# Four residual stages and an attention layer on one core: second sums computed already turned, adapters that hold the identity, and most value products moved to the end of the first part

## The chip, the cores and the metric

The kernel runs on one core of a Trainium2 chip. The metric is the device time of the whole kernel in microseconds (us). All numbers are float32. The engines are PE (TensorE, matrix products), DVE (VectorE), ACT (ScalarE), POOL (GpSimd) and SP (SyncE, which here only starts transfers). Each works through its own queue in order and waits on semaphores for the others.

## What is computed

The input x has 32 sequences of 32 rows of 512 numbers. Four residual steps follow each other:

```
x = x + mix(x)        # per sequence: a 32x32 matrix, picked by number, over the rows
x = x + x @ W.T + 0.5 * (x @ A[label]) @ Bw.T     # low rank 32, A picked among 5
x = x + x @ adapter[id].T                          # per sequence: a 512x512 matrix
x = x + attention(x)  # q, k, v projections, norm, rotation, cached pages, output
```

Below, x1, x2 and x3 are the values after the first, second and third step. The 1024 rows are handled as 8 tiles of 128 rows (4 sequences each).

## The kernel before

The kernel has three parts. The first makes x3 from x. The second makes queries, keys and values from x3; it goes by blocks of seven large products (`m`, L393) with everything around them on the other engines. The third is the attention. The change lies in the first part, and in the first chunk of value products (`project(NCH - 2, t)`, L312), which fill in there.

On PE a product needs the operand that is summed over on the partitions (the 128 rows of SBUF, the on-chip memory), so each x has to be had *turned*, with its 512 columns on the partitions in four pieces of 128 (`KC` = 4). In the first part PE does for each tile t:

- `mix(t)` (L688): four products of x with a 128x128 matrix `md` that holds the four sequences' mixing matrices and the identity. The result is x1 already turned (`x1t`); ACT copies it out of PSUM, the memory that PE writes.
- `low_1(t)` (L707): x1 times all five low-rank matrices `la`. DVE picks the tile's one (`picked`, L711, and a sum, L718) into `low`, a 128x128 tile of which 32 columns are used and the rest are zero.
- `base(t)` (L726): x1 times `wb`, which is W with the identity added on its diagonal (L850, four DVE adds at the start). It takes four matmuls of 512 columns, and gives x2 *not turned*, rows on the partitions. Ahead of the last one PE turns `low` (L729), ACT scales it by 0.5 (`lowt`, L731), and a fifth matmul of 512 columns (L732) adds the low-rank term with `lb`, of which 96 of 128 rows are zero. DVE copies the sum to `xs` (L734).
- `flip_2(t)` (L697): four transposes on PE that give `x2t`, and an ACT copy.
- `adapt(t)` (L751): 16 matmuls, for each of the four pieces one for each sequence, of 32 output rows beside each other, with the sequence's adapter `wa`, 1 MB each. DVE adds the result to `xs` (L758), which is x3.
- `transposed(t, x3t)` (L697): four transposes that turn x3, and an ACT copy. After each second tile POOL forms four sums of x3 (`token_sums`, L375 to L378) that the second part needs.

The tiles overlap: a loop over n gives `mix(n)`, `base(n-1)`, `flip_2(n-2)`, `low_1(n)`, the turning of x3 for tile n-4 and `adapt(n-3)`, and from n = 6 a value product of a finished tile. The order on PE and DVE in this part is that of the program text (`manual_schedule`); ACT, POOL and SP are ordered by the scheduler.

Adapters are loaded by SP, in order, into eight buffers (two tiles' worth). The loads of tile t+2 are issued after `adapt(t)`, which frees their buffers. Among them stand the weights of the value products (`wq`, after tile 3) and of the first pair of the second part (`w_pair`, after tile 5). SP's transfers use eight semaphores in turn, so that at most eight are under way.

`angles()` (L764 to L783) forms the angles of the rotation: some 18 DVE operations, three sines on ACT, and eight products on POOL (L789 to L792) into `cw` and `sw`, used from the second part's first block on. It stands right after `adapt(0)`. `constants()` (L136 and others) stands with it.

PSUM in this part: a pool `ps_m` of four banks, `ps_n` of two and `ps_tr` of two. `accumulator` gives every third sum of `base` and `adapt` to `ps_n`; `low_1` and the value products take `ps_m`. A new tile in a pool waits until the reader of the one that had its bank is done.

At the end of the part POOL stores `xs` to `x_d` (L891). Value products are copied out by ACT into two buffers (`vs`, L322) and stored from POOL's queue (L327).

## Time and profile before

| | us |
|---|---|
| median of 3 runs | 1136.51 |
| lowest and highest | 1135.58, 1136.70 |
| the profiled execution | 1136.3 |
| its span (first to last instruction) | 1134.5 |
| PE busy in the span | 1119.1 (99%) |
| DVE, ACT, POOL busy | 812.3, 739.3, 561.0 |
| start of the first product of the second part (`m`, L393) | 121.66 |
| `adapt(0)` to `adapt(7)` start on PE | 31.14, 42.17, 53.61, 64.64, 79.10, 95.01, 103.04, 114.11 |

The page gives busy time by engine, the span in 40 slices, the DMA queues, the chain of waits that ended last, the costliest groups of instructions, and the transfers. The time line lists instructions of an engine in order: start, duration, engine, line, operation, output and inputs, shape, and how many are merged in the row ("x8"; a float32 matmul is two entries). In square brackets stands how long the engine had been idle and what ended that. A matmul's listed duration overlaps the next, so its cost in a stream is read from the starts.

### The profile page before, as it was taken

What the parts mean: (1) busy time and instruction counts of PE and PEld (TensorE: products, weight loads), DVE (VectorE), ACT (ScalarE), POOL (GpSimd) and SP (SyncE); (2) the same over time, 40 slices, a digit from 0 to 9 for tenths busy, and PEclk for the clock granted to TensorE, in tenths of its full rate; (3) what the DMA queues carried; (4) which work ended last, traced back from release to release, by engine and by line L of the source; (5) the groups of instructions that cost most, each with busy time, mean ns of one, the idle gap of its engine ahead of it and who ended that gap; (6) DMA issues with size and microseconds to landing.
All of it is one profiled execution on the core that took longest, in us unless ns stands there. A gap on an engine that the chain in (4) does not pass through costs nothing.

```text
span 1134.5 us, 19093 instructions
## 1 busy us (share of the span) xinstructions
PE 1119.1 (99%) x5480; PEld 738.0 (65%) x5480; DVE 812.3 (72%) x1674; ACT 739.3 (65%) x1885; POOL 561.0 (49%) x730
## 2 busy tenths in 40 slices
PE   8999999999999899999999999999999999999998
PEld 5554444444444688777777777777777777777766
DVE  2510688887877578878778878887877787877861
ACT  1211377676666677678877777777777877777850
POOL 3411689899798455543444344334433443344410
PEclk9999999999999999999999999999999999999999
DMA  8998447688886687778767756775777676766600
GB/s 319 391 419 352 177 130 211 162 246 221 210 234 176 203 267 264 254 255 301 241 210 243 260 190 212 264 244 183 234 239 240 199 234 223 253 201 212 231 28 10
DMA packets 173355, 259.24 MB, mean 229 GB/s; under 512 B 31522, under 2 KB 130466, under 8 KB 168770
## 3 DMA queue, kind: packets, MB, share of 16 engines
q1 hardware_dynamic: 152226, 184.22, 51.4%
q0 software_dynamic: 20016, 71.97, 17.8%
q10 hardware_dynamic: 1008, 1.84, 0.4%
q8 instruction: 44, 0.72, 0.3%
q14 instruction: 61, 0.50, 0.1%
HBM read 228.46 MB, written 37.88 MB: 235 GB/s over the span
## 4 chain that ended last, share of the span: by engine, by line
PE 61%; DVE 2%; ACT 0%; issue 0%; DVEq 0%
PE o_ps L1103 19%; PE f_ps L1180 18%; PE s_ps L1023 11%; PE s_ps L1024 9%; PE o_ps L1123 2%; PE pn_ps L1090 1%; PE f_ps L1200 1%; PE f_ps_last L1200 1%; DVE placed L1079 1%; PE qkv L312 1%; DVE pr L1032 0%; DVE turned L1061 0%; ACT placed L1075 0%; DVE os L1139 0%; DVE ot L1160 0%
## 5 line engine op out<-in xcount | busy, mean ns | idle before, releaser
L1075 ACT COPY placed<-turned 32x512 f32<-32x512 f32 x524 | 322.6, 616 | 30.2 <-DVE turned L1061 24.2
L1103 PEld LDWEIGHTS o_ps<-vt,placed 128*128 128x128 f32 x2048 | 264.2, 191 | 110.9 <-issue 74.6
L1032 DVE CUSTOM_DVE_ANT_0 pr<-s_ps,mask,rq 128x544 f32<-128x544 f32 x256 | 200.4, 783 | 129.6 <-PE s_ps L1024 106.4
L1048 ACT ACTIVATE pr<-pr,low 128x544 f32<-128x544 f32 x256 | 191.6, 748 | 142.6 <-DVE low L1032 116.1
L1077 POOL COPY placed<-turned 32x512 f32<-32x512 f32 x279 | 169.6, 608 | 222.2 <-DVE turned L1061 173.5
L1103 PE MATMUL o_ps<-vt,placed 128*128 128x128 f32 x2048 | 272.0, 276 | 3.9 <-DVE os L1139 3.3
L1180 PE MATMUL f_ps<-wo,ot 128*128 128x512 f32 x480 | 240.6, 593 | 0.0
L1061 DVE STREAM_TRANSPOSE turned<-pr 128x512 f32<-128x512 f32 x256 | 178.6, 698 | 0.1
L1023 PE MATMUL s_ps<-kt,qt 128*128 128x288 f32 x512 | 174.0, 421 | 4.2 <-DVE low L1032 2.4
L1024 PE MATMUL s_ps<-kt,qt 128*128 128x256 f32 x512 | 152.3, 379 | 0.0
L252 POOL DMA_INDIRECT vt<-in_v_cache_dram,v_idx x128 | 124.3, 971 | 36.6 <-issue 25.7
L1024 PEld LDWEIGHTS s_ps<-kt,qt 128*128 128x128 f32 x512 | 97.3, 190 | 26.8
L438 POOL TENSOR_TENSOR ra<-ra,rs 128x512 f32<-128x512 f32 x80 | 103.8, 1303 | 10.7 <-DVE rs L433 8.1
L1079 DVE COPY placed<-turned 32x512 f32<-32x512 f32 x221 | 101.9, 461 | 5.6
L1180 PEld LDWEIGHTS f_ps<-wo,ot 128*128 128x128 f32 x480 | 86.9, 190 | 25.1 <-issue 13.9
L1086 POOL COPY pq<-pr 128x128 f32<-128x128 f32 x64 | 18.5, 288 | 151.6 <-ACT pr L1048 111.2
L1023 PEld LDWEIGHTS s_ps<-kt,qt 128*128 128x128 f32 x512 | 78.2, 191 | 17.3 <-DVE low L1032 6.1
L451 ACT ACTIVATE sq<-x 128x128 f32<-128x128 f32 x256 | 76.2, 301 | 19.8 <-DVE x L409 13.6
L548 ACT COPY r<-m 128x512 f32<-128x512 f32 x80 | 46.3, 579 | 52.4 <-PE m L393 50.4
L393 PE MATMUL m<-t_pair,x_sums 128*128 128x512 f32 x160 | 75.4, 594 | 0.7 <-ACT r L548 0.7
L393 PE MATMUL m<-w_pair,x3t 128*128 128x512 f32 x160 | 75.2, 592 | 0.0
L393 PE MATMUL m<-w_pair,x_sums 128*128 128x512 f32 x160 | 72.1, 593 | 0.0
(129 smaller groups left out, 1231.8 us busy)
## 6 DMA issues: line engine op xcount, KB each, us to landing
kt<-in_k_cache_dram SPq DMA_DIRECT2D x512, 128.0 KB
wa<-in_w_adapt_dram SPq DMA_DIRECT2D x32, 1024.0 KB
q_d<-st SPq DMA_DIRECT2D x128, 128.0 KB
qt<-q_d SPq DMA_DIRECT2D x64, 256.0 KB
w_pair<-in_w_qkv_dram SPq DMA_DIRECT2D x20, 512.0 KB
o_d<-in_w_o_dram SPq DMA_DIRECT2D x16, 512.0 KB
wo<-o_d SPq DMA_DIRECT2D x16, 512.0 KB
k_d<-st SPq DMA_DIRECT2D x32, 128.0 KB
```

The costliest lines, as they stand in the source:

```text
L252: nc.gpsimd.indirect_dma_start(out=vts[b][:, c, :], out_offset=None, in_=v_cache, in_offset=bass.IndirectOffsetOnAxis(ap=v_idx[:, at : at ...
L393: nc.tensor.matmul(ps, of[:, k], by[:, k], start=(not more and k == 0), stop=(k == KH - 1), skip_group_check=more,)
L1023: nc.tensor.matmul(ps[:, first:L], q, kt4[:, :N_LOW, g, :], start=True, stop=True)
L1024: nc.tensor.matmul(ps[:, L : first + LT], q, kt4[:, N_LOW:, g, :], start=True, stop=True)
L1032: nc.vector.tensor_tensor_reduce(pr, ps[:, first : first + LT], mask, rqs[b][:, g // QUAD, u : u + 1], 3.0e38, ALU.add, ALU.min, low,)
L1048: nc.scalar.activation(pr, pr, AF.Exp, bias=low, scale=-1.0, accum_out=dens[quad][:, u : u + 1])
L1061: nc.vector.transpose(part, pr)
L1075: nc.scalar.copy(dst, src)
L1077: nc.gpsimd.tensor_copy(dst, src)
L1079: nc.vector.tensor_copy(dst, src)
L1103: nc.tensor.matmul(po, pt[:, c, :], vt[:, c, g * D : (g + 1) * D], start=(c == 0 and q == 0), stop=(c == L // P - 1 and q == 1),)
L1180: nc.tensor.matmul(pfs[t][:, :HID], ots[t, h // HALF][:, h % HALF, :], wo(h), start=(h == 0), stop=(h == (HQ if t < NT - 1 else HALF) - 1),)
```

## The change

- `base(g)` works on two tiles at once with the operands exchanged: `wb` is loaded as the weights and x1 turned (256 columns, two tiles) streams. The result is x2 *turned*, in four banks of `ps_m`. `flip_2` and its four transposes per tile go; four ACT copies of 256 columns per pair make `x2t`.
- The low-rank term: `low` holds the 32 columns four times (one DVE copy more), turned and scaled for two tiles, and four matmuls, each with 32 rows of `lb` and of `lowt` at another partition (four row groups), add it to the four banks. `lb` comes in four transfers of 16 KB.
- Since x2 is no longer had with rows on the partitions, the adapters get the identity added: `with_identity(t)`, two DVE adds for each adapter (128x384 and 128x128), so that `adapt` gives x3 itself. DVE copies it to `xs`; the copy of x2 goes.
- The order is written out by hand. `angles()` moves from after `adapt(0)` to after `adapt(3)`, behind the adds of tile 4 and ahead of `mixed(6, 7)`. Of the value products one stands after `adapt(3)`, one after `adapt(4)`, the others after `adapt(6)` and `adapt(7)`. `wq` is loaded after tile 2's adapters, the first pair after tile 7's.
- `low_1`, `adapt` and the value products of this part now share the two banks of `ps_n`. Three memsets and that of `lb` go; `mg` and `md` have one buffer more.

On DVE the order around the moved part is: copy of `adapt(3)`, adds of tile 4, `angles`, picks of `low_1(6)` and `low_1(7)`, copy of `adapt(4)`, adds of tile 5. In `ps_n`, `adapt(4)` takes the bank of `low_1(6)`.

```diff
-        def base(t: int):
-            xt = x1ts.pop(t)
-            pb = accumulator(f"base_{t}")
-            for k in range(KC):
-                nc.tensor.matmul(pb, xt[:, k, :], wb[:, k, :], start=(k == 0), stop=False)
...
-            nc.tensor.matmul(pb, lowt, lb, start=False, stop=True)
-
-            nc.vector.tensor_copy(xs[:, t, :], pb)
-
-        def flip_2(t: int):
-            x2ts[t] = sp.tile([P, KC, P], F32, tag="x2t", name=f"x2t_{t}")
-            transposed(t, x2ts[t], "x2t")
+        def base(g: int):
+            xt = x1ts.pop(g)
+            pbs = [
+                ps_m.tile([P, HID], F32, tag="mm", name=f"base_{g}_{j}")[:, : 2 * P]
+                for j in range(KC)
+            ]
+            lowt = sp.tile([P, 2 * P], F32, tag="lowt", name=f"lowt_{g}")
+            for j in range(KC):
+                for k in range(KC):
+                    nc.tensor.matmul(
+                        pbs[j],
+                        wb[:, k, j * P : (j + 1) * P],
+                        xt[:, k, :],
+                        start=(k == 0),
+                        stop=False,
+                    )
+                if j == KC - 2:
+                    plt = ps_tr.tile([P, 2 * P], F32, tag="tr", name=f"lowt_ps_{g}")
+                    for u in range(2):
+                        low = lows.pop(2 * g + u).rearrange("p j r -> p (j r)")
+                        nc.tensor.transpose(plt[:, u * P : (u + 1) * P], low, ident)
                     nc.scalar.mul(lowt, plt, LORA_SCALING)
+            x2ts[g] = sp.tile([P, KC, 2 * P], F32, tag="x2t", name=f"x2t_{g}")
+            for j in range(KC):
+                r = slice(j * R, (j + 1) * R)
+                nc.tensor.matmul(pbs[j], lb[r, :], lowt[r, :], start=False, stop=True)
+            for j in range(KC):
+                nc.scalar.copy(x2ts[g][:, j, :], pbs[j])
...
+        def with_identity(t: int):
+            for b in range(t * BT, (t + 1) * BT):
+                w = was[b].rearrange("p k o -> p (k o)")
+                step = HID + P
+                most = w[:, : (KC - 1) * step].rearrange("p (k o) -> p k o", o=step)[:, :, :P]
+                last = w[:, (KC - 1) * step :]
+                one = ident.unsqueeze(1).to_broadcast([P, KC - 1, P])
+                nc.vector.tensor_tensor(most, most, one, ALU.add)
+                nc.vector.tensor_tensor(last, last, ident, ALU.add)
...
-            pa2 = accumulator(f"adapt_{t}")
+            pa2 = ps_n.tile([P, HID], F32, tag="mm", name=f"adapt_{t}")
...
-            nc.vector.tensor_tensor(xs[:, t, :], xs[:, t, :], pa2, ALU.add)
+            nc.vector.tensor_copy(xs[:, t, :], pa2)
...
+            base(0)
+            with_identity(0)
+            mixed(2, 3)
+            adapt(0)
+            loads(2)
...
+            base(2)
+            turned(2)
+            adapt(3)
+            loads(5)
+            with_identity(4)
+            values_of(0)
+            angles()
+            mixed(6, 7)
+            turned(3)
+            adapt(4)
+            loads(6)
+            with_identity(5)
+            values_of(1)
+            turned(4)
+            adapt(5)
+            loads(7)
+            with tc.issue_after(picked[-1]):
+                load_pair(0)
+            with_identity(6)
+            base(3)
+            turned(5)
+            adapt(6)
+            with_identity(7)
+            values_of(2)
+            values_of(3)
+            turned(6)
+            adapt(7)
+            values_of(4)
+            values_of(5)
+            turned(7)
+            values_of(6)
```

`mixed(6, 7)` is `mix` of both tiles and then `low_1` of both; `turned(t)` is the turning of x3 with POOL's sums after each odd tile; `values_of(t)` is a value product.

More of the change, by code (lines that the diff above doesn't have):

```diff
@@ L287, in cond_resid_kernel @@
     ps_tr = flips.enter_context(tc.tile_pool(name="a_tr", bufs=2, space=PSUM, side="right"))
-    taken = []
-    def accumulator(name: str, long: bool = False):
-        taken.append(name)
-        pool = ps_m if long or len(taken) % 3 else ps_n
-        return pool.tile([P, HID], F32, tag="mm", name=name)
     x3_all = xp.tile([P, KC, NT * P], F32, name="x3t")
@@ L327, in store_values, with project @@
         eng.dma_start(out=v_d[t * P : (t + 1) * P, c0 : c0 + HID], in_=vs)
-    def project(c: int, t: int, slots=()):
-        ps = accumulator(f"qkv_{c}_{t}", True)
+    def project(c: int, t: int, slots=(), pool=ps_m):
+        ps = pool.tile([P, HID], F32, tag="mm", name=f"qkv_{c}_{t}")
         for k in range(KC):
@@ L638, in cond_resid_kernel @@
         la = w1p.tile([P, KC, NL * R], F32, name="la")
-        lb = w1p.tile([P, HID], F32, name="lb")
-        nc.gpsimd.memset(lb, 0.0)
+        lb = w1p.tile([P, P], F32, name="lb")
         ones = w1p.tile([P, HID], F32, name="ones")
@@ L651, in cond_resid_kernel @@
         mgs, x1ts, lows, x2ts, was = {}, {}, {}, {}, {}
-        wide = [w1p.tile([P, P], F32, name=f"low_{i}") for i in range(3)]
-        for low in wide:
-            nc.gpsimd.memset(low, 0.0)
         def gather_mix(t: int):
-            mg = sp.tile([P, S], F32, tag="mg", name=f"mg_{t}", bufs=4)
+            mg = sp.tile([P, S], F32, tag="mg", name=f"mg_{t}", bufs=5)
             nc.gpsimd.indirect_dma_start(
@@ L670, in mixers @@
         def mixers(t: int):
-            md = sp.tile([P, BT, S], F32, tag="md", name=f"md_{t}", bufs=3)
+            md = sp.tile([P, BT, S], F32, tag="md", name=f"md_{t}", bufs=4)
             nc.vector.tensor_tensor(
@@ L690, in mix @@
                 )
-            x1ts[t] = sp.tile([P, KC, P], F32, tag="x1t", name=f"x1t_{t}", bufs=3)
-            nc.scalar.copy(x1ts[t], px)
+            g, u = divmod(t, 2)
+            if u == 0:
+                x1ts[g] = sp.tile([P, KC, 2 * P], F32, tag="x1t", name=f"x1t_{g}")
+            nc.scalar.copy(x1ts[g][:, :, u * P : (u + 1) * P], px)
         def transposed(t: int, dst: bass.AP, name: str):
@@ L704, in low_1 @@
         def low_1(t: int):
-            plo = ps_m.tile([P, HID], F32, tag="mm", name=f"low_ps_{t}")[:, : NL * R]
+            g, u = divmod(t, 2)
+            plo = ps_n.tile([P, HID], F32, tag="mm", name=f"low_ps_{t}")[:, : NL * R]
             for k in range(KC):
                 nc.tensor.matmul(
-                    plo, x1ts[t][:, k, :], la[:, k, :], start=(k == 0), stop=(k == KC - 1)
+                    plo,
+                    x1ts[g][:, k, u * P : (u + 1) * P],
+                    la[:, k, :],
+                    start=(k == 0),
+                    stop=(k == KC - 1),
                 )
@@ L716, in low_1 @@
             )
-            lows[t] = wide[t % 3]
+            lows[t] = sp.tile([P, KC, R], F32, tag="low", name=f"low_{t}")
             nc.vector.tensor_reduce(
-                lows[t][:, :R], picked.rearrange("p l r -> p r l"), AX.X, ALU.add
+                lows[t][:, 0, :], picked.rearrange("p l r -> p r l"), AX.X, ALU.add
             )
-        def base(t: int):
-            xt = x1ts.pop(t)
-            pb = accumulator(f"base_{t}")
-            for k in range(KC):
-                nc.tensor.matmul(pb, xt[:, k, :], wb[:, k, :], start=(k == 0), stop=False)
-                if k == KC - 2:
-                    plt = ps_tr.tile([P, P], F32, tag="tr", name=f"lowt_ps_{t}")
-                    nc.tensor.transpose(plt, lows.pop(t), ident)
-                    lowt = sp.tile([P, P], F32, tag="lowt", name=f"lowt_{t}")
-                    nc.scalar.mul(lowt, plt, LORA_SCALING)
-            nc.tensor.matmul(pb, lowt, lb, start=False, stop=True)
-            nc.vector.tensor_copy(xs[:, t, :], pb)
@@ L736, in flip_2 @@
-        def flip_2(t: int):
-            x2ts[t] = sp.tile([P, KC, P], F32, tag="x2t", name=f"x2t_{t}")
-            transposed(t, x2ts[t], "x2t")
+            nc.vector.tensor_copy(
+                lows[t][:, 1:, :], lows[t][:, 0, :].unsqueeze(1).to_broadcast([P, KC - 1, R])
+            )
[12 more added lines that the diff above has]
+                        xt[:, k, :],
+                        start=(k == 0),
+                        stop=False,
+                    )
+                if j == KC - 2:
[3 more added lines that the diff above has]
+                        nc.tensor.transpose(plt[:, u * P : (u + 1) * P], low, ident)
+                    nc.scalar.mul(lowt, plt, LORA_SCALING)
+            x2ts[g] = sp.tile([P, KC, 2 * P], F32, tag="x2t", name=f"x2t_{g}")
[4 more added lines that the diff above has]
+                nc.scalar.copy(x2ts[g][:, j, :], pbs[j])
@@ L742, in load_adapt @@
             dma_picked(was[b], w_adapt, pk[0:1, b : b + 1], "a p k o -> p (a k) o")
+        def with_identity(t: int):
[7 more added lines that the diff above has]
+                nc.vector.tensor_tensor(last, last, ident, ALU.add)
         def adapt(t: int):
-            xt = x2ts.pop(t)
-            pa2 = accumulator(f"adapt_{t}")
+            g, u = divmod(t, 2)
+            xt = x2ts[g][:, :, u * P : (u + 1) * P]
+            pa2 = ps_n.tile([P, HID], F32, tag="mm", name=f"adapt_{t}")
             for k in range(KC):
@@ L781, in angles @@
             nc.vector.scalar_tensor_tensor(turns, af, -1.0, af, ALU.mult, ALU.max)
-            cs = w1p.tile([P, NT, H2], F32, name="cs")
-            nc.scalar.activation(
-                cs.rearrange("p t f -> p (t f)"), turns, AF.Sin, bias=half_pi, scale=-1.0
-            )
+            cs = ang
+            nc.scalar.activation(af, turns, AF.Sin, bias=half_pi, scale=-1.0)
             for i in range(2):
@@ L803, in cond_resid_kernel @@
         load_x(2)
-        nc.sync.dma_start(out=lb[:R, :], in_=lora_b)
+        for j in range(KC):
+            nc.sync.dma_start(
+                out=lb[j * R : (j + 1) * R, :], in_=lora_b[:, j * P : (j + 1) * P]
+            )
         load_x(3)
@@ L827, in cond_resid_kernel, with mixed, ahead_of, loads @@
                 nc.tensor.matmul(idle[:, :n], ones[:, :P], ones[:, :n], start=True, stop=True)
-            def ahead_of(t: int):
-                if t + 3 < NT:
-                    gather_mix(t + 3)
-                if t < NT:
-                    mixers(t)
-            def adapt_and_load(t: int):
-                adapt(t)
-                if t + 2 < NT:
-                    for j in range(BT):
-                        load_adapt((t + 2) * BT + j)
+            def mixed(*tiles):
+                for t in tiles:
+                    mix(t)
+                for t in tiles:
+                    low_1(t)
+            def ahead_of(*tiles):
+                for t in tiles:
+                    if t + 3 < NT:
+                        gather_mix(t + 3)
+                    mixers(t)
+            def loads(t: int):
+                for j in range(BT):
+                    load_adapt(t * BT + j)
+            def turned(t: int):
+                transposed(t, x3t(t), "x3t")
+                if t % 2:
+                    token_sums(t // 2)
+            def values_of(t: int):
+                project(NCH - 2, t, (), ps_n)
             ahead_of(0)
@@ L852, in cond_resid_kernel @@
             low_1(1)
+            ahead_of(3)
             base(0)
-            mix(2)
-            low_1(2)
-            ahead_of(3)
-            flip_2(0)
-            base(1)
-            for n in range(3, NT + 4):
-                if n < NT:
-                    mix(n)
-                if n - 1 < NT:
-                    base(n - 1)
-                if n - 2 < NT:
-                    flip_2(n - 2)
-                if n < NT:
-                    low_1(n)
-                    ahead_of(n + 1)
-                if NT <= n:
-                    project(NCH - 2, n - 6 + (n == NT + 3))
-                if n == NT + 2:
-                    project(NCH - 2, NT - 3)
-                if 0 <= n - 4 < NT:
-                    transposed(n - 4, x3t(n - 4), "x3t")
-                    if n % 2:
-                        token_sums((n - 4) // 2)
-                if n - 3 < NT:
-                    adapt_and_load(n - 3)
-                if n == 3:
-                    constants()
-                    angles()
-                if 6 <= n < NT:
-                    project(NCH - 2, n - 6)
-                if n == 4:
-                    with tc.issue_after(picked[-1]):
-                        load_qkv(NCH - 2)
-                if n == 6:
-                    with tc.issue_after(picked[-1]):
-                        load_pair(0)
@@ new lines, in cond_resid_kernel @@
+            with_identity(0)
[3 more added lines that the diff above has]
+            with tc.issue_after(picked[-1]):
+                load_qkv(NCH - 2)
+            ahead_of(4, 5)
+            with_identity(1)
+            base(1)
+            turned(0)
+            adapt(1)
+            loads(3)
+            with_identity(2)
+            constants()
+            mixed(4, 5)
+            turned(1)
+            adapt(2)
+            loads(4)
+            ahead_of(6, 7)
@@ new lines, in cond_resid_kernel @@
+            with_identity(3)
+            base(2)
[14 more added lines that the diff above has]
+            loads(7)
+            with tc.issue_after(picked[-1]):
+                load_pair(0)
+            with_identity(6)
```

## The prediction

> **What bounds the kernel now.** I read the page first (PE 99% busy, the chain of waits almost all PE), then windows of 10 us over the first part, then the time lines of PE, DVE, POOL and SP there. Everything that the change touches lies before 121.66 us, where PE starts the first product of the next part (`m`, L393). From then on PE hardly pauses, so I count a shift of that moment one to one on the end.

> ```profile
> 60.00:70.00 10.00, 10.00 (x60) 4.73 (x59) 2.63 (x6) 1.45 (x3) 0.00 (x0) 1.00 1.02 421
> 70.00:80.00 10.00, 10.00 (x51) 5.75 (x53) 1.46 (x3) 2.62 (x5) 0.73 (x2) 1.00 1.00 417
> 80.00:90.00 10.00, 10.00 (x46) 4.03 (x39) 0.69 (x1) 0.86 (x2) 3.28 (x5) 1.00 1.02 419
> 90.00:100.00 10.00, 10.00 (x57) 4.29 (x56) 1.38 (x2) 2.25 (x4) 0.54 (x1) 1.00 0.85 329
> ```
> The columns are busy time of PE, PE's weight loads, DVE, ACT, POOL, then clock, DMA share and GB/s. Two things are full at once: PE (10.00 of 10.00) and the DMA engines (share 1.00, 417 to 421 GB/s). PE is the bound, but only just: tile 4's adapters have moved by 70 us and are used at 79.10. Work taken from PE soon runs into the loads, and DVE, nearly idle here, becomes the place where the change puts its new work.

> **PE: what is removed and added.** Start to start, in PE's time line: one 512-column pass is 0.43 us, and each fp32 matmul is two passes.

> ```profile
> 25.12 2.74 PE L726 MATMUL base<-wb,x1t 128*128 128x512 f32 x6
> 27.70 0.27 PE L729 MATMUL lowt_ps<-ident,low 128*128 128x128 f32 x1
> 27.81 1.02 PE L726 MATMUL base<-wb,x1t 128*128 128x512 f32 x2
> 28.67 1.02 PE L732 MATMUL base<-lb,lowt 128*128 128x512 f32 x2
> 29.52 0.60 PE L697 MATMUL x2t_ps<-ident,xs 128*128 128x128 f32 x4
> ...
> 402.13 0.73 PE L1123 MATMUL o_ps<-vn,pn 32*128 32x128 f32 x16
> 402.78 0.75 PE L1023 MATMUL s_ps<-kt,qt 128*128 128x288 f32 x2
> ```
> Before, a tile's `base` takes 25.12 to 29.52 = 4.40, and turning x2 another 0.44 (29.52 to 29.96): 9.68 for two tiles. After, two tiles take 16 matmuls of 256 columns (a half pass, 0.215 each, 32 passes: 6.88), two transposes (0.22) and four low-rank matmuls of 32 rows. Their nearest row is L1123, also four groups of 32 rows: 16 passes of 128 columns in 402.13 to 402.78 = 0.65, where one after another they would be 1.72. The low-rank four stream the same number of columns: 0.65, bounds 0.43 (all four beside each other) and 1.72 (none). Sum 7.75, so 1.9 less per pair and 7.7 over four pairs (3.4 to 8.6). If PE had no wait, that would be the gain. It has.

> **Loads.** A tile's four adapters are 4.19 MB, 10.0 us at 419 GB/s. In windows of 1 us, tile 2's last bytes move at 46.5 in before; the DMA was never idle until then, so an earlier request doesn't move it. A transfer counts as landed some 1 us after its bytes (adapter 3: its byte count is reached at 23.1, SP's next issue, which waits for it, is at 24.30). With no gap after that: `wq`, now right behind tile 2, 49.0; tile 3 bytes 59.0, landed 60.0; tile 4 landed 70.0; tile 5, with a 256 KB value store between, 80.6. Before had 1 to 2 us of gaps here, so this is already the better case.

> **PE against the loads.** The identity adds on DVE: the four independent 128x128 adds to `wb` (L850) take 0.90 together, a 128x512 add follows the next at 0.60, so 0.5 for the 128x384 one and 0.2 for the last: 0.7 per adapter, 2.8 per tile. Only the last adapter's 0.7 lies behind the landing. `adapt(0)` then comes at about 25 instead of 31.14, `adapt(2)` at 48.9 (landed 47.5, the adds, `v_idx` and a pick ahead of it in DVE's queue) instead of 53.61. Then 3.57 (`adapt`), 7.75, 0.5 (turning x3): `adapt(3)` 60.8, with its adapters there at 60.7. Value product 3.5, two `mix` 1.8, two `low_1` 2.4, turning 0.5: PE could begin `adapt(4)` at 72.6. The 7.7 us gained have become waits for loads, about 3.5 of them ahead of `adapt(2)`; the extra low-sum copies, the 16 KB `lb` pieces and the fewer POOL memsets all end in these waits and cost nothing.

> **DVE: the moved angles.** This decides. In DVE's queue of the changed kernel stand, in this order: copy of `adapt(3)`, the adds of tile 4 (they wait for its landing), all of `angles`, then the picks of `low_1(6)` and `low_1(7)`. `adapt(4)` takes the PSUM bank of `low_1(6)`, so it waits for that pick.

> ```profile
> 35.83 0.16 DVE L764 CAST pos<-ii 128x8 f32<-128x8 int32 x1
> 36.02 0.50 DVE L218 TENSOR_SCALAR mask<-key_i,len_f 128x544 f32<-128x544 int16 x1
> 36.70 1.39 DVE L768 TENSOR_SCALAR ang<-fr,pos 128x64 f32<-128x64 f32 x8
> ...
> 39.07 2.13 DVE L775 SCALAR_TENSOR_TENSOR ang<-turns,ang 128x512 f32<-128x512 f32 x3
> ...
> 41.70 0.69 DVE L781 SCALAR_TENSOR_TENSOR turns<-ang 128x512 f32<-128x512 f32 x1
> ...
> 43.62 1.18 DVE L674 TENSOR_TENSOR md<-mg,quarter 128x128 f32<-128x128 f32 x1
> 44.83 1.25 DVE L681 TENSOR_TENSOR md<-md,ident 128x128 f32<-128x128 f32 x1
> ...
> 124.21 4.32 DVE L367 TENSOR_TENSOR t_pair<-w_pair 128x512 f32<-128x512 f32 x1 [2.05 <-DMA w_pair<-in_w_qkv_dram]
> ```
> `angles` runs from 35.83 to 42.3, less 0.4 for the mask: 6.1 us. Before, it hid beside a 3.6 us `adapt` and a `base`. After: 70.0 + 0.7 (last adds) + 6.1 + 0.4 (pick) = 77.2, and about 0.7 more because POOL's sums of x3 (four of 0.73) now fall beside it: `adapt(4)` at 77.9, a wait of 5.3 us.

> **DVE against POOL.** The last three lines above show the second cost. A 128x128 add of two SBUF operands takes 0.29 alone (20.68), but 1.18 and 1.25 while POOL forms the angle factors, and a 128x512 one took 4.32 instead of 0.69 while POOL ran three operations. The eight factor products are 1.28 each:

> ```profile
> 45.89 1.32 POOL L791 TENSOR_TENSOR sw<-nsn,nw 128x512 f32<-128x512 f32 x1
> 47.17 1.27 POOL L789 TENSOR_TENSOR cw<-cs,nw 128x512 f32<-128x512 f32 x1
> ```
> They now run from 78 to 88.3. `adapt(4)` ends at 81.5, its copy at 82.4, and only then do the eight adds of tile 5 begin: alone they end at 85.2; one per POOL operation, about 88.8; shut out until POOL is done (as in the 4.32 row), 91.1. PE, past a value product and a turning, is ready at 85.5. I take 88.8, since the two rows of 1.2 are the same POOL products and the same kind of add. [...]

> **Sum.** From `adapt(5)` on no load is late: tile 7 lands near 106, is wanted near 112, and the pair weights, now requested after tile 7, land near 111, wanted at 116. So PE runs: `adapt` 3.57, `base(3)` 7.75, turning 0.5, `adapt` 3.57, two values 6.97, turning 0.5, `adapt` 3.57, two values 6.97, turning 0.5, value 3.5 = 37.4. The values moved to the end cost what they did before; they fill no wait that decides. 88.8 + 37.4 = 126.2 against 121.66: **+4.5 us**. The profiled execution took 1136.3 (span 1134.5 and 1.8 around it), the median of the three runs is 1136.51, so the difference is within their spread. Forecast 1136.3 + 4.5 = **1140.8**. Bounds: 85.5 and 91.1 for `adapt(5)` give +1.2 and +6.8; serial low-rank matmuls add 1.1 (only `base(3)` lies behind the last wait), full overlap takes 0.2.

> Two costs that the trace doesn't show. Between its first product and 121.66 PE never pauses over 0.7 us now; after, it stands for 3 to 5 us three times. Its very first 512-column passes take 0.95 (1.48 to 5.26, four of them), against 0.43 later; if a pause brought that back for the same 4 us, it costs 2 each time, at least 0. [...] The other: the store of xs now goes out ahead of two value stores on POOL's queue and takes 13.6 us to land, and value copy 6 on ACT waits for a store behind it. That is some 5 us late, but the first copy it holds up (`r`) is wanted 8.7 us after the first product: 0, at most 1.

> **Rivals.** (1) *The gain survives (faster):* the angles hide after all, since low_1(6) or tile 4 come early enough that the pick isn't last. Then `adapt(5)` waits only for tile 5, at 81.3 to 83.5: first product at 118.7 to 120.9, 1134.2 with 1133.3 to 1135.5. It decides if the pick is done by 72.6, 4.6 us ahead of my sum; DVE's order and the full DMA speak against. (2) *No exclusion on POOL:* adds at their lone speed, PE ready last: +1.2, 1137.5. It needs POOL's factors not to meet the adds; the 1.18 and 1.25 rows speak against. (3) *Worse:* adds shut out until 91.1 and a slow PE after the pauses: +6.8 and 2, 1145.

> **Numbers.** Forecast 0.55, rival 1 0.12, rival 2 0.18, rival 3 0.15. 0.2% is 2.3 us, about what a measurement of this kernel can tell from no change. Faster by more than that needs nearly all of rival 1's better half: 0.05. Within: the rest of rival 1 (0.07), rival 2 (0.18), and a little of the forecast: 0.27. Slower: 0.68. Range 1136.0 to 1144.8: it leaves out rival 1 and the upper half of rival 3.

> **What would show it.** DVE's time line: `angles` between 71 and 78 with the pick behind it; PE's wait ahead of `adapt(4)` near 5 us, put down to DVE; adds of tile 5 of over 1 us each beside POOL's factors; `adapt(5)` at 88 to 89; `m` first at 126. If `adapt(4)` starts by 74, my reading of the queue is wrong; if adds of 0.5 stand beside POOL's products, the exclusion is; if `base` for two tiles takes 8.8, the row groups don't overlap.

## The result and the profile after

The changed kernel takes 1145.11 us (median of 6 runs, 1142.43 to 1147.04) against 1136.16 for the kernel before (6 runs, 1135.57 to 1136.70): ratio 1.0081, 95% interval 1.0070 to 1.0092. It is slower, as forecast, but by 9 us and not by 4.5: the time lies just above the forecast's range. The profiled execution took 1144.81 (span 1142.0), the one before 1136.3 (span 1134.5).

The loss lies where it was looked for. The first `m` starts at 129.82 instead of 121.66, 8.2 us late, and the first score product of the attention at 381.49 instead of 373.7, 7.8 us late. All line numbers of the changed kernel are its own: `low_ps` is L697, `base` L728, the low-rank products L744, `adapt` L770, the picks L705, the adds L759 and L760, the angles L783 to L800, the factor products on POOL L806 to L809.

PE's time line after (start, duration, and in brackets the wait):

```profile
19.78 0.71 PE L744 MATMUL base<-lowt,lb 32*128 32x256 f32 x8
...
27.28 5.34 PE L770 MATMUL adapt<-wa,x2t 128*32 128x512 f32 x32 [2.58 <-DVE picked L705]
...
50.61 3.64 PE L770 MATMUL adapt<-wa,x2t 128*32 128x512 f32 x32 [1.16 <-DVE picked L705]
...
80.35 6.13 PE L770 MATMUL adapt<-wa,x2t 128*32 128x512 f32 x32 [5.85 <-DVE picked L705]
86.41 3.70 PE L304 MATMUL qkv<-wq,x3t 128*128 128x512 f32 x8
...
90.48 5.14 PE L770 MATMUL adapt<-wa,x2t 128*32 128x512 f32 x32
```

PE, which had no pause over 0.7 us in this part before, now waits three times for a pick, 5.85 us at the worst. And the products behind two of these waits are slow: the 16 `adapt` matmuls of a tile (32 entries) take 3.57 us start to start where PE comes to them without a pause, and still do behind the wait of 1.16, but 5.27 from 27.28 and 6.06 from 80.35 to 86.41. The windows of 1 us show why (columns as in the prediction; the third number from the end is the clock):

```profile
77.00:78.00 1.00, 0.00 (x0) 0.00 (x0) 1.00 (x1) 0.00 (x0) 1.00 (x2) 1.00 1.03 434
78.00:79.00 1.00, 0.00 (x0) 0.00 (x0) 0.93 (x3) 0.04 (x1) 0.92 (x2) 0.79 0.98 410
...
82.00:83.00 1.00, 1.00 (x12) 0.28 (x8) 0.06 (x1) 0.00 (x0) 1.00 (x2) 0.50 0.00 0
...
84.00:85.00 1.00, 1.00 (x8) 0.20 (x4) 0.00 (x0) 0.00 (x0) 1.00 (x2) 0.50 0.00 0
85.00:86.00 1.00, 1.00 (x12) 0.12 (x4) 0.00 (x0) 0.00 (x0) 1.00 (x1) 0.79 0.00 0
```

DVE's time line after shows what PE waited for (the last row is POOL's, at the same time):

```profile
75.12 2.95 DVE L794 SCALAR_TENSOR_TENSOR ang<-turns,ang 128x512 f32<-128x512 f32 x3
...
79.99 0.31 DVE L705 TENSOR_TENSOR picked<-low_ps,which 128x160 f32<-128x160 f32 x1
...
86.64 0.69 DVE L777 COPY xs<-adapt 128x512 f32<-128x512 f32 x1 [4.58 <-PE adapt L770]
87.25 0.55 DVE L759 TENSOR_TENSOR wa<-wa,ident 128x384 f32<-128x384 f32 x1
87.71 1.35 DVE L760 TENSOR_TENSOR wa<-wa,ident 128x128 f32<-128x128 f32 x1
88.99 1.61 DVE L759 TENSOR_TENSOR wa<-wa,ident 128x384 f32<-128x384 f32 x1
...
88.88 1.31 POOL L808 TENSOR_TENSOR sw<-nsn,nw 128x512 f32<-128x512 f32 x1
```

The angles run from 72.29 to 80.0 and the pick stands behind them. The adds of tile 5 take up to 1.35 (128x128) and 1.61 (128x384) beside POOL's factor products, which end at 90.2, and 0.28 and 0.55 without them.

### The profile page after: what moved, and what is told of

It reads as the page before. It is cut to its first block, busy times and chain, and to the rows that moved or that the text cites. A ratio compares the mean times of both kernels' runs of the same rounds, so it can differ in the third digit from the quotient of the medians.

```text
span 1142.0 us, 19255 instructions
## 1 busy us (share of the span) xinstructions
PE 1118.9 (98%) x5528; PEld 748.8 (66%) x5528; DVE 829.0 (73%) x1738; ACT 738.9 (65%) x1889; POOL 562.0 (49%) x726
## 4 chain that ended last, share of the span: by engine, by line
PE 60%; DVE 2%; ACT 0%; issue 0%; DVEq 0%
PE o_ps L1149 19%; PE f_ps L1226 18%; PE s_ps L1069 11%; PE s_ps L1070 9%; PE o_ps L1169 2%; PE pn_ps L1136 1%; PE f_ps L1246 1%; PE f_ps_last L1246 1%; DVE placed L1125 1%; PE qkv L304 1%; DVE pr L1078 0%; DVE turned L1107 0%; ACT placed L1121 0%; DVE os L1185 0%; DVE ot L1206 0%
## 5 line engine op out<-in xcount | busy, mean ns | idle before, releaser
L1123 POOL COPY placed<-turned 32x512 f32<-32x512 f32 x279 | 169.6, 608 | 221.5 <-DVE turned L1107 172.9
```

The lines of the kernel that those rows point to most:

```text
L1123: nc.gpsimd.tensor_copy(dst, src)
```

## The experiments

Theory at the start: the place of the angles decides, with a slow clock and a late start of the adapters on top. Rivals: one of those two alone, or the adds themselves. Every ratio below is to the kernel before, run beside it on the same chip (it took 1138.61 beside runs 1 to 4, 1130.85 beside runs 5 to 8, 1131.14 beside runs 9 to 11, 1130.92 beside the last two). Runs of different groups, and the changed kernel itself, are compared by these ratios alone.

### 1. Angles early (e1_angles_early)

```diff
             adapt(0)
             loads(2)
+            constants()
+            angles()
...
-            constants()
...
             values_of(0)
-            angles()
             mixed(6, 7)
```

> Changed kernel with constants and angles back where they were, right after adapt(0), and nothing else. Theory (the picks of low_1(6) stand behind the angles in DVE's queue, and the angles behind tile 4's landing): the wait ahead of adapt(4) goes (adapt(4) at about 74.4 instead of 80.35), the clock stays full there, adapt(5) waits only for tile 5 (about 83), first product m at 120.8 instead of 129.8, time about 1135.5 to 1136. Rival (the adds or the loads cost the time wherever the angles stand): m stays at 127 or later, time 1142 or more.

Measured: 1145.34, ratio 1.0068 [1.0051, 1.0085]. Nearly nothing came back, so the angles' place alone, as first stated, is not the cause. The wait at `adapt(4)` is gone, but the POOL products that follow the angles now meet the adds of tile 1. DVE in this run:

```profile
39.83 1.62 DVE L759 TENSOR_TENSOR wa<-wa,ident 128x384 f32<-128x384 f32 x1
41.37 1.35 DVE L760 TENSOR_TENSOR wa<-wa,ident 128x128 f32<-128x128 f32 x1
...
48.25 1.61 DVE L759 TENSOR_TENSOR wa<-wa,ident 128x384 f32<-128x384 f32 x1
49.79 0.28 DVE L760 TENSOR_TENSOR wa<-wa,ident 128x128 f32<-128x128 f32 x1
```

The eight adds take 10.2 us (39.83 to 50.0) where they need 2.7 without POOL. PE takes `adapt(1)` in bits between them, from 41.55 to 55.40, at a clock of 0.50 from 44 to 53. The price had not gone, it had moved.

### 2. PE kept busy ahead of adapt(4) (e2_kept_busy)

```diff
+            for n in range(6):
+                nc.tensor.matmul(hot, ones[:, :P], ones, start=True, stop=True)
             adapt(4)
```

> Changed kernel with six products of ones, 512 columns each (5.2 us), put ahead of adapt(4), where PE stands for 5.85 us. They compute nothing that is used. Theory (the pause halves the granted clock from 78.8 to 85.8, and adapt(4) takes 6.06 instead of 3.57): adapt(4) takes 3.6 at clock 1.00; of the 2.5 us about half is lost again, since the adds of tile 5 then meet more of POOL's factor products; m at 128 to 128.6, 1143.5. If the slow adapt(4) had another cause, it stays at 6 us and the time at 1145 or more.

Measured: 1146.93, ratio 1.0074 [1.0057, 1.0090]: no gain. The trace says that this run could not tell. The six products took PE until 82.98, 2.9 us past the end of the pick, so `adapt(4)`, now 3.57 long, ended at 86.55 against 86.41 in the changed kernel: the filling spent what the clock gave. And in this execution `adapt(2)` had a pause of 4.37 and took 6.20. Runs 10 to 13 settle the question, in the version of run 7.

### 3. No adds (e3_no_adds)

The adds are left out, so that x3 lacks x2.

```diff
-            with_identity(0)
...
-            with_identity(7)
```

> Changed kernel without the adds of the identity to the adapters, so that x2 is left out of x3. Theory (queue order): without the adds nothing ahead of the angles waits for tile 4, the angles run from 67 to 73.5, the pick is done before PE is ready at 74.4, adapt(5) at 82.2 when tile 5 has landed, m at about 120.1, time about 1135. Rival (angles cost their 6 to 8 us on PE wherever they stand in that stretch): adapt(4) at 78 or later, time 1142.

Measured: 1136.38, ratio 0.9978 [0.9968, 0.9988]. Near what was expected. PE's time line has one row with a wait left, and no pause at `adapt(4)`, although the angles stand at their late place:

```profile
49.03 3.62 PE L770 MATMUL adapt<-wa,x2t 128*32 128x512 f32 x26 [1.44 <-DMA wa<-in_w_adapt_dram]
...
73.14 3.64 PE L770 MATMUL adapt<-wa,x2t 128*32 128x512 f32 x32
...
119.51 1.88 PE L385 MATMUL m<-w_pair,x3t 128*128 128x512 f32 x4
```

Without adds nothing on DVE waits for a landing, the angles begin at 65.7 right behind the copy of `adapt(3)`, and the picks are there when PE is. So the adds are the step that ties picks, angles and copies to the transfers. And even free of them the change is worth only 2.2 us at `m` (119.51 against 121.66), of the 6.8 that PE's own work shrank by (9.68 before, 7.97 measured after, four pairs).

### 4. lora_b in one transfer (e4_lb_one)

```diff
-        for j in range(KC):
-            nc.sync.dma_start(out=lb[j * R : (j + 1) * R, :], in_=lora_b[:, j * P : (j + 1) * P])
+        nc.sync.dma_start(out=lb, in_=lora_b)     # lora_b is handed in as 128x128
```

> Changed kernel with lb laid out by rows of its four groups, so that one transfer brings it in place of four. Theory (the three extra issues hold SP, the first adapter is requested at 11.71 instead of 9.46, and the DMA engines are part idle from 12 to 15, so every later tile lands 1.6 to 1.9 us late): tile 0 complete at 24.4, tile 4 at 69.8, adapt(4) at about 78.5, m at 128, time 1143.2. Rival (the loads are not on the path): no change, 1145.

Measured: 1147.62, ratio 1.0082 [1.0065, 1.0099]: missed, and no different from the changed kernel's 1.0081. The adapters did start earlier (first issue 9.06 against 11.71), `adapt(0)` came at 24.62 without a wait and at full rate. But tile 2's last piece landed at 48.05, against 49.27, and with PE that much earlier the wait ahead of `adapt(2)` was 4.83 and its products slow. PE in this run:

```profile
49.92 6.35 PE L770 MATMUL adapt<-wa,x2t 128*32 128x512 f32 x32 [4.83 <-DVE picked L705]
...
78.80 5.34 PE L770 MATMUL adapt<-wa,x2t 128*32 128x512 f32 x32 [2.27 <-DVE picked L705]
...
91.61 4.29 PE L770 MATMUL adapt<-wa,x2t 128*32 128x512 f32 x28 [1.76 <-DVE wa L759]
```

The adds of tile 5 then met the POOL products in full (84.89 to 92.4, 7.5 us). What is gained in one place becomes a longer wait in the next as long as the picks stand behind adds that wait for a landing.

### 5 and 6. POOL's products away (e6_products_late), and the angles early as well (e7_early_and_late)

The second theory: two things together, the angles in front of the picks and POOL's products beside the adds; moving one leaves the other. The eight products go to DVE, behind the last tile's adds; in the second run the angles stand behind the adds of tile 1 too.

```diff
-                nc.gpsimd.tensor_tensor(cw[:, i, :, :H2], cs, w1, ALU.mult)
+                nc.vector.tensor_tensor(cw[:, i, :, :H2], cs, w1, ALU.mult)   # and the other three
...
             with_identity(7)
+            trig_factors()
```

> Edit: the eight products that make the sine and cosine factors are taken from GpSimd and put on VectorE behind the last tile's adds; the angles stay where they are. Theory A (what makes the adds dear is that GpSimd's products lengthen them wherever the two meet): the adds of tile 5 take 0.84 us a piece, 3.4 in all instead of 4.9, and adapt(5) starts as soon as TensorE is there, near 89 us; adapt(4) still waits 5 to 6 us for the pick behind the angles and still runs at half the clock; m near 128, so about 1 to 1.5 us below the changed kernel, ratio to before 1.006. Rival B (the adds are late only because the angles stand ahead of them): no difference from the changed kernel.

Measured: 1136.74, ratio 1.0048 [1.0031, 1.0065]. The time is a little better than expected. The adds of tile 5 take 2.8 us (86.25 to 89.0), `adapt(5)` starts at 89.49 without a wait, `m` at 127.34. The wait ahead of `adapt(4)` is not the 5 to 6 us forecast, because PE had waited 4.51 ahead of `adapt(2)` and came late; its products are slow all the same:

```profile
80.16 5.33 PE L770 MATMUL adapt<-wa,x2t 128*32 128x512 f32 x32 [2.27 <-DVE picked L705]
```

> Edit: as in the run with the products late, and the angles stand behind the adds of tile 1. Theory A: neither the picks of tiles 6 and 7 nor any add is held up now; what is left are the waits for the last piece of tile 0 and of tile 2 with the picks queued behind it (1 to 3 us each, some of it at half the clock); m between 121 and 124, ratio to before 1.000 to 1.002. Rival B (the price is the adds' own 27 us on VectorE, or the start): m above 126, ratio 1.004 or more.

Measured: 1130.40, ratio 0.9994 [0.9984, 1.0003]: the whole loss is gone, `m` starts at 120.83. PE in this run has `adapt(4)` and `adapt(5)` without a wait:

```profile
75.30 3.64 PE L770 MATMUL adapt<-wa,x2t 128*32 128x512 f32 x32
78.87 3.70 PE L304 MATMUL qkv<-wq,x3t 128*128 128x512 f32 x8
82.41 0.60 PE L686 MATMUL x3t_ps<-ident,xs 128*128 128x128 f32 x4
82.94 3.69 PE L770 MATMUL adapt<-wa,x2t 128*32 128x512 f32 x32
```

By the ratios the products' place is worth 0.33% of the time (1.0081 to 1.0048, about 3.7 us) and the angles' place, once the products are away, 0.54% (1.0048 to 0.9994, 6.1 us). With the products still on POOL the angles' place was worth 0.13% (1.0081 to 1.0068), within the intervals. The adds as such cost little then: what remains against the run without adds is 0.16%, and the two intervals overlap.

### 7 and 8. base one step ahead (e8_base_ahead, e9_base_ahead_lb_one)

In e7 PE still waits ahead of `adapt(0)` (2.46) and `adapt(2)` (2.86). PE has work that it could do there: the next pair's `base`.

```diff
             base(0)
             with_identity(0)
             mixed(2, 3)
+            base(1)
             adapt(0)
...
             mixed(4, 5)
             turned(0)
+            constants()
+            angles()
             adapt(1)
...
+            base(2)
             turned(1)
             mixed(6, 7)
             adapt(2)
```

The value products behind `adapt(3)` to `adapt(7)` are spread differently too.

> Edit: products late and angles early as before, and on TensorE each pair's base is taken one step earlier, so that a tile's adapters have landed and have their identity when its adapt comes up (order: base(0), mixes of 2 and 3, base(1), adapt(0), mixes of 4 and 5, adapt(1), base(2), mixes of 6 and 7, adapt(2) and on, base(3) ahead of adapt(4)). Theory A: TensorE waits nowhere over 1 us between 18 us and m, no stretch at half the clock; m at 118 to 120 against 121.7 in the kernel before, ratio 0.997 to 0.999. Rival B (the tiles' landing, a ring of two tiles freed by adapt, becomes the bound when adapt comes later): transfers pause, waits at adapt(4) to adapt(7), m at 122 or later, ratio 1.001 or more.

Measured: 1127.31, ratio 0.9964 [0.9950, 0.9978]; clock 1.000 in the profiled execution. This version is faster than both kernels, by 0.36% of the one before. Its first `m`, at 113.24, can't be set against the forecast, since here it stands ahead of two value products; the one behind them starts at 122.36, in run 6 at 125.98. One wait above 1 us is left, and no slow row:

```profile
31.98 3.64 PE L770 MATMUL adapt<-wa,x2t 128*32 128x512 f32 x32
37.03 2.05 PE L675 MATMUL x1t_ps<-md,xs 128*128 128x128 f32 x16 [1.41 <-DVE md L668]
```

The rival, transfers that pause because `adapt` frees buffers later, did show (DMA share 0.74 in 60 to 70), but cost PE little: 0.44 us ahead of part of `adapt(5)`.

> Edit: as the run before, and lora_b arrives in one transfer of 64 KB that is laid out for it (the host only permutes the input). If issue on SyncE ahead of the first adapters still matters, m is 1 to 1.5 us earlier than in the run before; if TensorE is the bound there, the two are equal within 0.3 us.

Measured: 1127.76, ratio 0.9965 [0.9953, 0.9978]: equal, so the issue on SP ahead of the first adapters doesn't matter once PE is the bound.

### 9. The products on GpSimd again (e12_products_gpsimd)

The version of run 7 with one thing put back: POOL's products right behind the angles.

```diff
             angles()
+            trig_factors()      # on gpsimd
             adapt(1)
...
-            trig_factors()      # on vector, behind with_identity(7)
```

> Edit: the version with base ahead, but its eight sine and cosine products are on GpSimd again, right behind the angles (near 49 us), where they meet the adds of tile 2. Theory A (the products lengthen the adds that they meet, and those hold the picks and mixers behind them): adds of tile 2 take 8 to 11 us in place of 3.4, adapt(2) waits 3 to 6 us, some of it paid again in clock; 3 to 9 us over the version with base ahead, ratio to before 0.999 to 1.005. Rival B (with base ahead there is slack enough): within 1 us of it, ratio 0.996 to 0.998.

Measured: 1136.97, ratio 1.0055 [1.0039, 1.0070]: 0.9% (10 us) dearer than run 7, just past the upper end of what theory A gave. DVE's adds of tile 2 run from 50.21 to 61.1, the mixers of tiles 6 and 7 follow until 64.1, and PE waits 8.23 us for the first of them (done at 62.56; the row names no releaser), then works at a clock of 0.50 until 68.7:

```profile
59.75 1.34 DVE L760 TENSOR_TENSOR wa<-wa,ident 128x128 f32<-128x128 f32 x1
...
62.66 3.75 PE L675 MATMUL x1t_ps<-md,xs 128*128 128x128 f32 x16 [8.23 <-issue]
```

Here nothing else changed, so the cost of the two engines meeting, the pause and the slow products behind it included, is shown by itself.

### 10 to 13. What a pause costs PE (e10_pause, e11_pause_filled, e13_short_pause, e14_short_filled)

Idle passes on DVE make PE pause once, ahead of `adapt(4)` of the version of run 7; in the second of each two the pause is to be covered by six idle products, as in run 2.

```diff
-            with_identity(4)
+            with_identity(4, (1, 2, 3))
+            for n in range(24):                   # 13 in the second two
+                nc.vector.tensor_scalar(trig[3], trig[3], 1.0, None, ALU.mult)   # trig[3] is turns
+            with_identity(4, (0,))
```

> Edit: the version with base ahead, with 24 idle passes of VectorE (0.43 us each, 10.3 us) between the adds of tile 4's pieces 1 to 3 and the add of piece 0, so that TensorE pauses once, about 6 us, ahead of adapt(4). Theory A (a pause of 5 to 6 us is paid twice, once as itself and again as products at half the clock): adapt(4) takes about 6.1 us in place of 3.64, and the time is that of the run with the pause filled plus 2.5 us. Rival B (the slow rows in the changed kernel are the profile's or something else's): equal to the run with the pause filled within 0.5 us.

> Edit: the same pause for adapt(4), filled on TensorE by six idle products of ones (12 passes of 512 columns, 5.3 us). Theory A: adapt(4) at the same place, 3.64 us, granted clock 1.00; 2.5 us below the run with the bare pause and about 6 us over the version with base ahead. Rival B: equal to the bare pause.

Measured: 1138.58 (1.0063 [1.0050, 1.0076]) and 1138.99 (1.0064 [1.0051, 1.0077]), equal. Not a verdict for B: a pass took 0.53 us and not 0.43, the pause came out at 10.86, and with the filling still at 5.74; `adapt(4)` was slow in both, 4.93 and 6.11. The next two have 13 passes.

> Edit: as the run with the pause, but 13 idle passes of VectorE instead of 24, since each took 0.53 us and not 0.43 and the pause came out at 10.9 us. The pause ahead of adapt(4) should be 5.1 us. Theory A (slow products behind a pause are paid on top of it): adapt(4) takes 5.3 to 6.2 us in place of 3.64; 1.7 to 2.5 us more than with the pause filled; about 7 us over the version with base ahead. Rival B (the slow rows cost nothing in the end, hidden by a later wait): equal to the filled one.

> Edit: the same, with six idle products of ones (5.3 us) on TensorE ahead of adapt(4), so that the pause is covered. Theory A: adapt(4) at 3.64 us and a granted clock of 1.00 throughout, m 1.7 to 2.5 us earlier than with the bare pause. Rival B: equal to it.

Measured: 1133.80 (1.0028 [1.0018, 1.0038]) and 1131.40 (1.0007 [0.9998, 1.0016]), 2.4 us apart. PE with the bare pause, and after it with the filled one:

```profile
84.45 5.53 PE L770 MATMUL adapt<-wa,x2t 128*32 128x512 f32 x32 [5.87 <-DVE wa L759]
```

```profile
84.10 3.64 PE L770 MATMUL adapt<-wa,x2t 128*32 128x512 f32 x32 [0.65 <-DVE wa L759]
```

`adapt(4)` begins at nearly the same moment and takes 5.46 in the one and 3.57 in the other; `m` starts at 120.01 and 117.90. So this pause of 5.9 us costs itself and some 2 us more in slow products, and nothing later hides it. Theory A holds; the bare pause is 0.64% (7 us) over run 7, as forecast.

## Why the prediction was right in kind and too small

The mechanism on record holds in its parts: PE's saving turns into waits, the pick behind the angles holds `adapt(4)`, and POOL's products stretch the adds of tile 5. Runs 5, 6 and 9 show the two places as causes. Two terms that the sum put at nothing failed: the later start of the loads (+1.6) and the slow products behind the pauses (+2.5, of which 1.7 came back in the adds). Point by point, with `m` at 129.82 where the sum had 126.2:

- **PE's work**: 7.75 per pair, measured 7.97 (95.55 to 103.52); the low-rank group 0.65, as predicted (19.78 to 20.43), where one after another they would take 1.72 (eight passes of 0.215, an estimate from the same time line): the row groups do work beside each other. Right within 0.2.
- **Loads: a step that failed.** The step "the 16 KB `lb` pieces ... cost nothing" had them end in a wait that was there anyway. The first adapter is issued at 11.71 instead of 9.46, behind their four issues, and in each 10 us window from 20 to 70 us the DMA share is 1.01 or more, so nothing makes up for it: `adapt(2)` at 50.61 instead of 48.9, tile 4's last add done at 72.29 instead of 70.7, **+1.6**. The prediction argued that an earlier request moves nothing while the DMA is never idle; it did not look at a later first request. Run 4 shows that with the pieces gone the adapters do come earlier (tile 2's last by 1.2 us), but the kernel is no faster: the delay is measured, and it is no cause that can be removed by itself.
- **Angles**: 6.1 and 0.7 for POOL's sums; measured 7.7, **+0.9**. The contention was seen but taken too small: the three L794 rows took 2.95 instead of 2.13, L795 0.83 instead of 0.43 and L800 1.10 instead of 0.69. The pick so came at 80.0 and `adapt(4)` at 80.35, 2.4 past the sum's 77.9. The wait itself, forecast at 5.3, was 5.85.
- **Slow products behind a pause: the other step that failed.** The prediction named it, gave it "2 each time, at least 0", and put it into the sum at 0 because the profile of before has no pause. `adapt(4)` took 6.06 instead of 3.57, **+2.5**, the largest single term of what was missing. Runs 12 and 13 measure 2.1 at `m` and 2.4 in the whole time for such a pause. In the changed kernel a faster `adapt(4)` would not have given the 2.5 back, though: in run 4 it ended 2.3 us earlier (84.07 instead of 86.41), tile 5's adds met more of POOL's products (which ended at 91.1 there), and `adapt(5)` ended at 95.83 instead of 95.55. That trade is the -1.7 of the next item, and what is left of the term on the path is about 0.8, less than the late loads cost. Behind the shorter pauses the price was 1.7: `adapt(0)` took 5.27 instead of 3.57 behind 2.58 us here, `adapt(4)` 5.27 behind 2.27 us in run 4.
- **DVE against POOL**: forecast 3.6 us over the adds' own time. Since `adapt(4)` ended 4.9 late and POOL's products only 1.9 late (90.2 instead of 88.3), the adds met the tail of them only; `adapt(5)` ended at 95.55, 3.2 past the sum's 92.4, **-1.7** against the 4.9. The mechanism is shown by run 9; what the products put on top of a tile's adds, 2.8 us alone, was 2.1 here, 4.8 in run 4, 7.5 in run 1 and 8.1 in run 9.
- **The rest**: 34.27 from there to `m` instead of 33.83, **+0.4**. Together +1.6 +0.9 +2.5 -1.7 +0.4 = 3.7, against the 3.6 to explain.
- **ACT's value copies**: copy 6 waited 6.77 us for a store, as foreseen, and PE didn't wait for it. Right.

These terms are those of one execution of each kernel, whose spans differ by 7.5 us (1142.0 and 1134.5). The medians differ by 9: the six runs of the changed kernel spread over 4.6 us, those of before over 1.1, and one profile can't say what pauses the longer runs had.

Of the rivals the third, "adds shut out and a slow PE", gave the right time (1145) for half of the right reason: the slow PE was there, the adds were not shut out. The range ended at 1144.8, because it left out the upper half of the one rival that priced the slow products, although the forecast itself had three pauses.

## What to carry to other kernels

Where a step's saving turns into waits on the same engine, price the pauses themselves: behind the bare pause of 5.87 us in run 12 `adapt(4)` took 5.46 instead of 3.57, filling the pause (run 13) gained 2.4 us, and against run 7, which has no such pause, it cost 7 us, more than its length (run 7 put products that were due anyway into the last two waits, spread the value products anew and gained another 0.3% on run 6). When a new operation waits for a transfer, what stands behind it in its engine's queue inherits that wait (here the angles began at 72.29, when tile 4's last add was done, and the pick behind them at 79.99; without the adds, in run 3, at 65.7 and 71.80); look for what other engines need from that queue. And a cost that follows an operation, here POOL's products behind the angles, moves with it: moving only the operation ahead may pay the same bill at the next place (run 1: the adds of tile 1 took 10.2 us instead of 2.7).

## What the runs showed of the hardware

- **The low clock came in stretches of 3.4, 6.8 and 10.2 us.** Worked out from the 1 us windows (a window at 0.79 is 0.42 of it at 0.50): 78.6 to 85.4 in the changed kernel (6.8), 80.2 to 83.6 in e6 (3.4), 26.2 to 29.6 in e7 (3.4), 82.0 to 92.3 in e10 (10.2), 87.8 to 94.7 in e11 (6.8), 81.5 to 88.3 in e13 (6.8). In these six it begins 2.0 to 4.1 us after PE stopped. What a pause cost in slow products went with how much of the stretch lay behind it: e10's, after a pause of 10.86, ended 2.8 us after `adapt(4)` began and cost 1.4 us (4.93 instead of 3.57), e11's, after one of 5.74, ended 5.2 us after it and cost 2.5 (6.11).
- **The length of a pause alone did not decide.** Pauses of 2.27 (e4), 2.46 (e7) and 2.58 (after) brought the low clock, one of 2.86 (e7, ahead of `adapt(2)`) and one of 2.30 (e2) did not. What decided was not shown. Where a run has two low stretches and the windows give both starts, these are 51.2 us apart in the changed kernel (27.39 and 78.59, from 0.5 us windows), 30.7 in e6 (49.48 and 80.20) and 30.7 in e4 (48.6 and 79.3, from 5 us windows): 15 and 9 times 3.41, but three pairs make no rule. Nearly the same pause cost 1.7 us or nothing: `adapt(0)` takes 5.27 in the changed kernel (pause 2.58) and 3.57 in run 2 (pause 2.30), which is the same program up to there.
- **DVE and POOL slow each other.** An add of two SBUF operands takes 1.61 instead of 0.55 (128x384) and 1.35 instead of 0.28 (128x128) beside POOL's products, while these go from 1.26 (after, 82.39, DVE idle) to 1.58 (e1, 40.99) and POOL's sums from 0.73 to 1.17 (after, 75.22). A row with one tensor operand was slowed too: L795 took 0.83 instead of 0.43 beside POOL's sums. In e1 adds and products started in turn: the adds 1.54 and 1.27 us apart (39.83, 41.37, 42.64), and so the products (40.99, 42.53, 43.80). The 4.32 row of before, beside three POOL operations, does not fit that.
